# A streaming residual kernel: rows of x read in runs of 16 KB and stored from runs of 8 KB

## The chip, the cores and the metric

The kernel runs on one core of a Trainium2 chip (trn2). The metric is the device time of one execution in microseconds (us); lower is better. The kernel before took 329.73 us, the median of three runs (329.72 to 330.26). All data are float32 in the chip's memory at the start and must be there at the end.

## The reference

There are 128 samples. Each sample is a matrix x[b] of 128 channels by 1024 time steps, and a subject number from 0 to 7 picks one of eight 128 x 128 weight matrices for it:

```python
w = weights[subjects]                            # (128, 128, 128)
out = jnp.einsum('bct,bcd->bdt', x, w)
return x + out                                   # (128, 128, 1024)
```

x is 64 MiB and so is the output; the weights are 0.5 MiB. Every byte of x is read once, and every byte of the output is written once.

## The kernel before, in words

The kernel works on pairs of samples (`G = 2`), so there are `NT = 64` steps. On-chip memory holds 23 slots (`SLOTS`, the tiles `xs`) of one pair each: 128 partitions by 2 x 1024 floats, 1 MB. Channel c of both samples lies in partition c. A step loads a pair into a slot, adds the products to it in place, and stores the slot.

Each engine has its own list of instructions, written out by hand in one critical section; semaphores alone order the engines among each other.

- **SyncE (SP)** issues the 64 loads (L92), in order. From the 24th on it first waits on `s_store[k]` (L91), until the slot's former content has been stored. At the end it waits for the last stores (L138).
- **ScalarE (ACT)** issues the load of the 128 subject numbers (L74), that of all eight weight matrices into `w_all` (L75), and then the 64 stores (L132), each after both samples of its step have been added (`s_added`). Loads are thus on SP's DMA queue (q1 in the profile) and stores on ACT's (q10), with the weights at the head of q10.
- **VectorE** brings the subject numbers into range (L80 to L84), and then makes one addition per sample (L128): product from PSUM plus the slot's content, into the slot.
- **GpSimd (POOL)** waits for the weights (L96), reads a sample's subject number into a register and copies that matrix into one of four small tiles `w0` to `w3` (L112), for each sample in turn.
- **TensorE (PE)** waits for the load of the step (`s_load[k]`, L99) and for the copied matrix (`s_copied`), and multiplies in two halves of 512 columns (L118) into one of four PSUM tiles. Nothing can be multiplied before the weights are there.

A load's access pattern is `"g c t -> c g t"`: for each of 128 partitions two rows of 4 KB, which lie 512 KB apart in memory. The store's pattern is the same in the other direction. Each row is one packet of a DMA engine, and the 128 partitions are spread over the core's 16 DMA engines.

## Time and profile before

| | value |
|---|---|
| median of the runs | 329.73 us |
| the profiled execution's own time | 329.91 us |
| its span, first to last instruction | 328.1 us |
| mean granted TensorE clock | 0.972 |
| TensorE / VectorE / GpSimd busy | 71% / 48% / 12% of the span |
| moved by DMA | 134.86 MB in 35,867 packets, 411 GB/s over the span |
| load of 1 MB, issue to landing (median) | 32.9 us |
| store of 1 MB, issue to landing (median) | 32.3 us |

The span lies inside the run's time; 1.8 us of the profiled execution are outside it. Busy times overlap, since the engines work side by side. The profile's second part cuts the span into 40 slices of 8.2 us and gives each engine's busy share in tenths. Its line DMA is the mean busy share of the 16 DMA engines, and GB/s is what they moved. An issue-to-landing time includes the wait behind earlier transfers of the same queue.

### The profile page before, as it was taken

Reading aid. Unit: us, or ns where it says so; the run is one execution under the profiler, and the core shown is the slowest. Engines: PE = TensorE matmul, PEld = TensorE weight load, DVE = VectorE, ACT = ScalarE, POOL = GpSimd, SP = SyncE. Lnnn points to the kernel's source line nnn. Section 1 sums busy time; section 2 is a strip of 40 time slices with the busy share of each in tenths; the row PEclk is TensorE's granted clock in tenths of the full one; section 3 lists DMA queues with packets and bytes.
Section 4 is the critical chain, followed back from the end, with each engine's and each line's share of the span. In section 5 each row is a group of like instructions: output and inputs, shape, how many; then the busy total and the mean of one; then the engine's idle time right before and its main releaser. Section 6 shows DMA issues by size and latency. Waiting matters only on the chain.

```text
span 328.1 us, 1864 instructions
## 1 busy us (share of the span) xinstructions
PE 233.1 (71%) x512; PEld 94.5 (29%) x512; DVE 157.5 (48%) x131; POOL 37.8 (12%) x132
## 2 busy tenths in 40 slices
PE   0069999999997768768668668677677686686200
PEld 0034444444432322323323223223223233232000
DVE  0017777777775454454454454454554544544200
POOL 0011111111111111111111111111110111110000
PEclk9999999999999999999999999999999999999855
DMA  7999999999999999999999999999999999999995
GB/s 270 391 407 413 422 420 419 423 417 420 423 419 419 422 419 419 420 422 420 420 422 420 421 420 420 420 421 422 419 421 422 417 421 422 421 419 423 421 418 239
DMA packets 35867, 134.86 MB, mean 411 GB/s; under 512 B 2065, under 2 KB 3090, under 8 KB 35858
## 3 DMA queue, kind: packets, MB, share of 16 engines
q10 hardware_dynamic: 18450, 67.64, 50.4%
q1 hardware_dynamic: 17408, 67.11, 50.2%
q8 instruction: 4, 0.07, 0.1%
q14 instruction: 5, 0.04, 0.0%
HBM read 67.63 MB, written 67.11 MB: 411 GB/s over the span
## 4 chain that ended last, share of the span: by engine, by line
SPq 81%; DMA 10%; PE 1%; issue 1%; DVE 0%
SPq L92 81%; DMA x<-in_x_dram 10%; PE ps L118 1%; DVE x L128 0%; SPq L162 0%; SPq L72 0%
## 5 line engine op out<-in xcount | busy, mean ns | idle before, releaser
L118 PE MATMUL ps<-x,w 128*128 128x512 f32 x512 | 233.1, 605 | 72.4 <-DMA x<-in_x_dram 53.3
L128 DVE TENSOR_TENSOR x<-ps,x 128x1024 f32<-128x1024 f32 x128 | 156.8, 1225 | 147.0 <-PE ps L118 147.0
L118 PEld LDWEIGHTS ps<-x,w 128*128 128x128 f32 x512 | 94.5, 191 | 210.2 <-issue 122.1
L112 POOL COPY w<-w_all 128x128 f32 x128 | 37.6, 294 | 257.9 <-PE ps L118 239.2
L80 DVE TENSOR_SCALAR near<-given 1x128 int32<-1x128 int32 x1 | 0.2, 215 | 2.2 <-DMA given<-in_itok_B_dram 2.2
L84 DVE CUSTOM_DVE_ANT_0 index<-near,wrap 1x256 uint16<-1x256 uint16 x1 | 0.3, 280 | 0.0
L82 DVE TENSOR_SCALAR wrap<-near 1x128 int32<-1x128 int32 x1 | 0.2, 216 | 0.0
L153 POOL MEMSET const-float32-0.0<- 128x1 f32 x1 | 0.1, 98 | 0.2 <-issue 0.2
L153 POOL MEMSET const-bfloat16-1.0<- 128x1 bf16 x1 | 0.1, 101 | 0.0
L153 POOL MEMSET const-uint8-127<- 128x1 uint8 x1 | 0.1, 101 | 0.0
L153 POOL MEMSET const-float32-1.0<- 128x1 f32 x1 | 0.1, 98 | 0.0
## 6 DMA issues: line engine op xcount, KB each, us to landing
x<-in_x_dram SPq DMA_DIRECT2D x64, 1024.0 KB, 32.9
out_dram<-x ACTq DMA_DIRECT2D x64, 1024.0 KB, 32.3
w_all<-in_L_cond_weights_dram ACTq DMA_DIRECT2D x1, 512.0 KB, 16.5
given<-in_itok_B_dram ACTq DMA_DIRECT2D x1, 0.5 KB
```

The lines of the kernel that those rows point to most:

```text
L80: nc.vector.tensor_scalar(near, given, -S, S - 1, ALU.max, ALU.min).then_inc(s_index, 1)
L82: nc.vector.tensor_scalar(wrap, near, 0, S, ALU.is_lt, ALU.mult).then_inc(s_index, 1)
L84: nc.vector.tensor_tensor(index, near, wrap, ALU.add).then_inc(s_index, 1)
L92: nc.sync.dma_start(xs[k], x[i * G : (i + 1) * G].rearrange("g c t -> c g t")).then_inc(s_load[k], DMA)
L112: nc.gpsimd.tensor_copy(w, w_all[:, bass.ds(s, 1), :]).then_inc(s_copied, 1)
L118: mm = nc.tensor.matmul(p[:, t : t + N], w[:, 0, :], xs[k][:, g, t : t + N], start=True, stop=True,)
L128: nc.vector.tensor_tensor(xs[k][:, g, :], p, xs[k][:, g, :], ALU.add).then_inc(s_added, 1)
L153: nc = _bacc.Bacc("TRN2", target_bir_lowering=False, num_devices=1)
```

## The change

Loads and stores are built by a new helper, `transfer`, that hands the two sides' access patterns to the instruction as they are, so that the side that is read and the side that is written can be cut into runs of different length.

- **Loads.** There is one load per sample in place of one per pair, so 128 of 512 KB. The source is seen as 32 runs of four rows (`ROWS = 4`), 16 KB each; the destination is still 128 partitions with a row of 4 KB each. Both loads of a slot count on the same semaphore, and matmul waits for both.
- **Stores.** There are still 64 of 1 MB. The source, a slot, is seen as one run of 8 KB per partition (both samples); the destination is still two rows of 4 KB per partition.
- **Allocation.** Tiles come from raw allocations in place of pools.

The loads of the subject numbers and of the weights are as before.

```diff
+ROWS = 4
+QUEUES = {mybir.EngineType.SP: "qSPDynamicHW", mybir.EngineType.Activation: "qActDynamicHW"}
+
+
+def transfer(nc, engine, out, in_):
+    later, nc._always_lower_symbolic_ap = nc._always_lower_symbolic_ap, False
+    ins, outs = engine.lower_ap_dma(in_), engine.lower_ap_dma(out)
+    nc._always_lower_symbolic_ap = later
+    return engine.add_instruction(
+        mybir.InstDMACopy(
+            name=nc.get_next_instruction_name(),
+            engine=engine.engine,
+            ins=ins,
+            outs=outs,
+            mode="Copy",
+            cce_op=ALU.bypass,
+            queue=QUEUES[engine.engine],
+        )
+    )
...
-    xs = [pool.tile([C, G, T], F32, name=f"x{i}") for i in range(SLOTS)]
-    ps = [psum.tile([D, T], F32, name=f"ps{i}") for i in range(P_SLOTS)]
+    xs = [sbuf(f"x{i}", C, G, T) for i in range(SLOTS)]
+    ps = [
+        ctx.enter_context(nc.psum_tensor(f"ps{i}", [D, T], F32)).ap() for i in range(P_SLOTS)
+    ]
...
             if turn:
                 nc.sync.wait_ge(s_store[k], DMA * turn)
-            nc.sync.dma_start(
-                xs[k], x[i * G : (i + 1) * G].rearrange("g c t -> c g t")
-            ).then_inc(s_load[k], DMA)
+            for g in range(G):
+                transfer(
+                    nc,
+                    nc.sync,
+                    xs[k][:, g, :],
+                    x[i * G + g].rearrange("(a r) t -> a (r t)", r=ROWS),
+                ).then_inc(s_load[k], DMA)
...
-            nc.tensor.wait_ge(s_load[k], DMA * (turn + 1))
+            nc.tensor.wait_ge(s_load[k], DMA * G * (turn + 1))
...
-            nc.scalar.dma_start(
-                out[i * G : (i + 1) * G].rearrange("g d t -> d g t"), xs[k]
+            transfer(
+                nc,
+                nc.scalar,
+                out[i * G : (i + 1) * G].rearrange("g d t -> d g t"),
+                xs[k].rearrange("d (o g) t -> d o (g t)", o=1),
             ).then_inc(s_store[k], DMA)
```

More of the change, by code (lines that the diff above doesn't have):

```diff
@@ L49, with sbuf @@
     NT = B // G
-    pool = ctx.enter_context(tc.tile_pool(name="pool", bufs=1))
-    psum = ctx.enter_context(tc.tile_pool(name="psum", bufs=1, space=bass.MemoryType.PSUM))
-    given = pool.tile([1, B], I32, name="given")
-    near = pool.tile([1, B], I32, name="near")
-    wrap = pool.tile([1, B], I32, name="wrap")
-    index = pool.tile([1, B], I32, name="index")
-    w_all = pool.tile([C, S, D], F32, name="w_all")
-    ws = [pool.tile([C, 1, D], F32, name=f"w{i}") for i in range(W_SLOTS)]
-    xs = [pool.tile([C, G, T], F32, name=f"x{i}") for i in range(SLOTS)]
-    ps = [psum.tile([D, T], F32, name=f"ps{i}") for i in range(P_SLOTS)]
+    def sbuf(name, *shape, dtype=F32):
+        return ctx.enter_context(nc.sbuf_tensor(name, list(shape), dtype)).ap()
+    given, near, wrap, index = (
+        sbuf(name, 1, B, dtype=I32) for name in ("given", "near", "wrap", "index")
+    )
+    w_all = sbuf("w_all", C, S, D)
+    ws = [sbuf(f"w{i}", C, 1, D) for i in range(W_SLOTS)]
+    xs = [sbuf(f"x{i}", C, G, T) for i in range(SLOTS)]
+    ps = [
+        ctx.enter_context(nc.psum_tensor(f"ps{i}", [D, T], F32)).ap() for i in range(P_SLOTS)
+    ]
     s_given = tc.alloc_semaphore("s_given")
```

## The prediction

> **What bounds the kernel now.** I read the slices first, then the queues, the chain, the groups and the stage table.

> ```profile
> PEclk9999999999999999999999999999999999999855
> DMA  7999999999999999999999999999999999999995
> GB/s 270 391 407 413 422 420 419 423 417 420 423 419 419 422 419 419 420 422 420 420 422 420 421 420 420 420 421 422 419 421 422 417 421 422 421 419 423 421 418 239
> ...
> q10 hardware_dynamic: 18450, 67.64, 50.4%
> q1 hardware_dynamic: 17408, 67.11, 50.2%
> q8 instruction: 4, 0.07, 0.1%
> q14 instruction: 5, 0.04, 0.0%
> ...
> SPq 81%; DMA 10%; PE 1%; issue 1%; DVE 0%
> ```

> The 16 DMA engines are full in all slices but the first and the last, at 417 to 423 GB/s from the fifth slice on. q1 carries the loads and q10 the stores, and their packets fill 100.6% of the engines' time. The chain lies on SP's queue (81%), which is SP being held in its load instructions until the engines make room. So the span is bytes divided by rate.

> ```profile
> L118 PE MATMUL ps<-x,w 128*128 128x512 f32 x512 | 233.1, 605 | 72.4 <-DMA x<-in_x_dram 53.3
> L128 DVE TENSOR_TENSOR x<-ps,x 128x1024 f32<-128x1024 f32 x128 | 156.8, 1225 | 147.0 <-PE ps L118 147.0
> ...
> w_all<-in_L_cond_weights_dram ACTq DMA_DIRECT2D x1, 512.0 KB, 16.5
> ```

> The stage table's columns are busy time by engine, the TensorE clock, the DMA share and GB/s:

> ```profile
> 18.00:27.00 9.00, 7.87 (x14) 3.54 (x15) 3.02 (x3) 2.05 (x7) 1.00 1.02 409
> 27.00:60.00 33.00, 33.00 (x78) 14.63 (x77) 23.66 (x20) 5.59 (x19) 1.00 1.03 420
> 100.00:200.00 100.00, 74.45 (x162) 28.94 (x161) 49.43 (x41) 11.76 (x40) 1.00 1.02 420
> 299.00:324.00 25.00, 5.20 (x12) 1.82 (x10) 4.71 (x4) 0.00 (x0) 0.71 1.03 421
> 324.00:329.00 5.00, 0.00 (x0) 0.00 (x0) 0.00 (x0) 0.00 (x0) 0.50 0.11 44
> ```

> TensorE is full from 27 to 60 us, while it works off the loads that came in before the weights, then 74% busy. While it catches up, VectorE's adds start every 1.716 us, so compute takes 3.43 us for a slot of two samples; a load and a store of a slot take the DMA 4.99 us. Compute is 30% faster than what binds.

> **One packet's price.** The trace records each packet. With 4 bytes (a semaphore's increment) it lasts 9.0 ns, with 512 bytes (weights) 27.9, with 4 KB 159.1: a line of 0.0366 ns per byte over 9 ns. Four instruction fetches of 8 KB amid the full traffic took 309 ns, as the line says (300 + 9). Records overlap their neighbours, so the occupancy is less: from 60 to 290 us there are 23,589 packets of 4 KB, 1,481 of 4 bytes, and fetches. 230 us x 16 engines, less 1,481 x 9 ns and 5 us of fetches, over 23,589 gives 155.2 ns; the commonest distance between packet starts is 155.3. The bytes cost 150.0 of that, so each packet costs 5.3 ns beside its bytes.

> [...]from 20 to 28 us (4 us bins on the trace's own zero, 12.3 us before the span's) there are 338 load packets of 4 KB per 354 weight packets of 512 B.

> **The change, part by part.**
> (1) Loads. 1 MB is 64 KB for each engine: 16 packets of 4 KB now, 4 of 16 KB after. The bytes, and the rows that one engine takes, are the same. If a packet is what is read as one run, 12 packets x 5.3 ns = 64 ns are saved per load. 16 KB isn't in the trace as an x transfer: by the line it takes 600 + 5.3 = 605 ns.
> (2) Stores. 16 packets become 8 of 8 KB: 8 x 5.3 = 42 ns. Bounds for (1) and (2) together: zero, if the cost is per written row (rows stay 4 KB on both sides); 20 x 9 = 180 ns per pair if the whole 9 ns goes. I take 106, because the 8 KB fetches follow the line.
> (3) One more load instruction per slot: a further 4-byte packet per engine, +9 ns. SP's extra issue is at least 0.42 us (shortest load issue), 64 x 0.42 = 27 us in all; it hides under SP's being held, median 4.63 us an issue. Uncovered it would cost those 27 us.
> Per pair 106 - 9 = 97 ns; 64 pairs make -6.2 us.
> (4) Turns. Weights have 64 packets of 512 B per engine, each taking turns with one load packet. With 605 in place of 155 ns they land 64 x 0.45 = 28.8 us later, at 47 instead of 18 us; the first matmul moves from 19 to 48, the first store's issue from 26 to 55. What covers it is slots: 23 MB at about 2.47 us each last to about 60 us, and longer once stores take turns. Compute then needs 64 x 3.43 = 220 us and ends by 268, well before the end. Without this cover (a smaller number of slots) the delay would stop the DMA. What I charge is 28 us more of the loads-only stretch, which runs at 409 instead of 420 GB/s: 2.6%, +0.7 us.
> (5) Loads at 16 KB a turn against 8 KB for stores win 2:1 until all slots are out, then SP waits on `s_store`. The next loads queue behind that wait and matmul waits for them; but then some twenty finished or unfinished slots lie between, stores are always queued, and the engines stay full. After the last load the stores' tail grows from about 10 slots to some 20; it runs at 421 GB/s, so it costs nothing.
> (6) Raw allocation instead of pools, and the doubled wait count for a load: no instruction on PE, DVE, ACT or POOL is added, and matmuls wait in the same places. Nothing, under the full DMA.

> Sum against the profiled execution: 328.1 - 6.2 + 0.7 = 322.6 us of span; with the 1.8 us outside it (329.9 - 328.1) 324.4. The profiled run lies 0.2 us above the median of 329.73. I forecast 324.5.

> **Rivals.**
> *The price is per written row.* [...]Then nothing is saved and the third semaphore packet is paid: 64 x 9 ns = +0.6, 330.4 us. The same holds if the hardware cuts the runs back to rows.
> *Long packets are slow (slower).* For: the trace's four 16 KB packets[...] took 878 to 960 ns instead of the line's 609, and the 4 KB packets after them 441 and 260. Against: [...]8 KB fetches in the same traffic took 309. At 919 ns a load is 4 x 919 - 4 x 605 = 1.26 us dearer: +80 us, 404. It decides from a 16 KB packet of 605 + 97/4 = 629 ns on, 4% above mine; a mild form, 640 ns, gives 324.4 + 64 x 4 x 0.035 = 333 us.
> *The late weights uncover the DMA.* For: 55 us to the first store's issue, against 60 to the last free slot, and stores need 9.2 us to land. Against: 23 slots, and stores fill the engines once they start. A gap of 3 us gives 327.5. TensorE would bind only if it needed over (319 - 48) / 64 = 4.2 us a slot; the clock stayed at 1.00 from 27 to 290 us.

> **How the numbers follow.** Savings per packet, forecast 324.5 (322 to 327[...], with part of a gap): 0.60. Larger, because the loads-only stretch also speeds up (down to 320.5): 0.06. Gap or part of the savings lost, 327 to 329: 0.06. Per written row, 330.4: 0.13, of which two thirds within 0.2%. Slow long packets: 0.15. About 0.2% (0.7 us) is what a measurement tells from no change. So faster 0.71, same 0.10, slower 0.19. The range 321.0 to 331.5 leaves out the slow packets, and the largest gains.

> **What would show it.** Loads' packets should number 4,096 of 16 KB plus 2,048 semaphores, stores' 8,192 of 8 KB plus 1,024; if rows are recorded instead, the GB/s line decides, which I expect at 428 to 430. The weights' time to landing should go from 16.5 to about 45 us; were it to stay, the turns are still 4 KB and the first rival gains. TensorE should be idle until about 48 us and near full until about 268; SP should wait on the stores. A rate below 420 in the mixed stretch, or load records above 629 ns, would make the forecast wrong, as would an empty DMA slice near 60 us.

## The result, and the profile after

The changed kernel takes 328.10 us (median of four runs, 327.64 to 328.31) against 329.76 us: a ratio of 0.9944, with a 95% interval of 0.9927 to 0.9962. It is faster by 0.56%, where 1.6% was forecast. Its profiled execution took 328.1 us with a span of 326.3, so the span is 1.8 us shorter than before; the forecast was 5.5.

The page of the changed kernel, with the lines that answer to those shown before (slices, queues, chain, TensorE, DMA issues):

```profile
PE   0499999999999888999989887775979877000000
...
DMA  7999999999999999999999999999999999999993
GB/s 268 407 416 422 420 425 419 425 426 423 429 425 421 427 422 428 419 427 424 419 426 420 428 422 434 417 429 423 425 429 426 427 420 425 427 426 427 428 424 164
...
q10 hardware_dynamic: 10258, 67.64, 49.6%
q1 hardware_dynamic: 6144, 67.12, 49.1%
...
x<-in_x_dram SPq DMA_DIRECT2D x128, 512.0 KB, 21.4
out_dram<-x ACTq DMA_DIRECT2D x64, 1024.0 KB, 42.2
w_all<-in_L_cond_weights_dram ACTq DMA_DIRECT2D x1, 512.0 KB, 10.0
```

The change did what it says. q1 now has 6,144 packets (4,096 of 16 KB and 2,048 semaphore increments), where its 17,408 of before were 16,384 rows of 4 KB and 1,024 increments, 16 to a load; and q10 has 8,192 packets of 8 KB beside the weights. The rate rose, but only to about 424 GB/s in the mixed stretch, where I expected 428 to 430. TensorE starts earlier and not later (first matmul at 12.7 us, before at 19.1). And the last slice fell from 239 to 164 GB/s in a span that is shorter: the DMA engines stop further apart than before.

The stage table shows that end best (columns: busy time by compute engine, TensorE clock, DMA share, GB/s). Before:

```profile
318.00:320.00 2.00, 0.00 (x0) 0.00 (x0) 0.00 (x0) 0.00 (x0) 0.50 1.03 424
320.00:322.00 2.00, 0.00 (x0) 0.00 (x0) 0.00 (x0) 0.00 (x0) 0.50 1.03 424
322.00:324.00 2.00, 0.00 (x0) 0.00 (x0) 0.00 (x0) 0.00 (x0) 0.50 1.03 422
324.00:326.00 2.00, 0.00 (x0) 0.00 (x0) 0.00 (x0) 0.00 (x0) 0.50 0.25 102
```

After:

```profile
318.00:320.00 2.00, 0.00 (x0) 0.00 (x0) 0.00 (x0) 0.00 (x0) 0.50 0.97 410
320.00:322.00 2.00, 0.00 (x0) 0.00 (x0) 0.00 (x0) 0.00 (x0) 0.50 0.56 234
322.00:324.00 2.00, 0.00 (x0) 0.00 (x0) 0.00 (x0) 0.00 (x0) 0.50 0.09 37
```

Before, the engines are full until 324 us. After, they begin to run dry at 320, but from 322 to 324 a share of 0.09, which is one and a half engines of 16, still works, and the kernel waits for it.

The trace's packet records give this engine by engine. They do not name the engine, but they fall into 16 sequences in which nearly every packet starts 3 to 4 ns before the record ahead of it ends (99.9% of the packets before and 99.8% after, from 60 to 290 us). Each sequence is taken as one engine and followed back from its last store. The table has the time of an engine's last packet, on the span's clock (to about 0.1 us). The median engine is the middle one of the 16 by that time. "Late" is the last engine less the median one.

| kernel | median engine, us | last engine, us | late, us |
|---|---|---|---|
| before | 324.15 | 325.68 | 1.5 |
| changed | 320.78 | 324.20 | 3.4 |

The median engine is done 3.4 us earlier, the last one only 1.5. In both kernels nine engines end within 0.4 us of each other and seven come later, so the median is one of those that did not lag. There are thus two shortfalls: the packets saved 3.4 us and not 6.2, and 1.9 us of that was lost to engines that lag.

**The packets' price.** The commonest distance between packet starts on one engine is 307 ns for 8 KB stores (most lie between 306 and 310), where two packets of 4 KB took 2 x 155.3 = 310.6, and 613 ns for 16 KB loads beside stores, where four took 621.2. With the bytes at 0.0366 ns (150, 300 and 600 ns) a packet of 4 KB cost 5.3 ns beside its bytes, one of 8 KB 7, one of 16 KB 13. So a longer packet was cheaper per byte (0.0379, 0.0375 and 0.0374 ns), but a part of the price came back as it grew: about a third of what merging two packets should have saved, and half with four. Per pair a load saves 4 x 8.2 = 33 ns, a store 8 x 3.6 = 29, and the extra semaphore costs 9: 53 ns x 64 = 3.4 us, as the median engine has it.

**The lag.** The DMA engines also carry the instruction fetches, packets of 8 KB (queue q14) and 16 KB (q8), eight in mid-run before and nine after. A fetch took time of its own on its engine, and the packet behind it took longer as well. Before, a 16 KB fetch took 878 to 960 ns and the next packet on that engine 441 instead of 159. After, it took 972 to 1,096 ns and a store's packet behind it about 700 instead of 311, or, in one case, a load's packet 1,153 instead of 616. The 8 KB fetches took about 310 ns in both; after, a load's packet behind one took 936 to 1,280 ns. By these records one fetch cost its engine 0.5 to 1.3 us before and 0.5 to 1.6 after. The engines were full from 27 to 318 us (a DMA share of 1.03 before, 1.01 after), so that there was no idle time in which to make that up.

Added up over all fetches this is 7.7 us before; the seven late engines ended together 7.7 us later than the mean of the other nine, so the fetches account for the whole of that lag, and none of it was made up. After, it is 9.4 us, and the late engines' sum is 12.3. Where the other 2.9 us come from stays open.

My theory for the experiments (A) was these two points: packets save less than forecast, and fetches make single engines late. The rivals: each packet saves its 5.3 ns and the gain is lost in the loads-only stretch (B in the first four runs; later B says that fetches don't matter); loads now run up to 23 slots ahead, and the long tail of stores alone loses the gain (C). The slots that loads are ahead of stores are called their lead below.

### The profile page after: what moved, and what is told of

The parts are those of the page before. It is cut to its first block, busy times and chain, and to the rows that moved or that the text cites. A ratio compares the mean times of both kernels' runs of the same rounds, so it can differ in the third digit from the quotient of the medians.

```text
span 326.3 us, 1928 instructions
## 1 busy us (share of the span) xinstructions
PE 237.0 (73%) x512; PEld 97.1 (30%) x512; DVE 157.5 (48%) x131; POOL 37.8 (12%) x132
## 3 DMA queue, kind: packets, MB, share of 16 engines
q10 hardware_dynamic: 10258, 67.64, 49.6%
q1 hardware_dynamic: 6144, 67.12, 49.1%
HBM read 67.63 MB, written 67.11 MB: 413 GB/s over the span
## 4 chain that ended last, share of the span: by engine, by line
DMA 37%; another core or an unknown queue 22%; PE 17%; SPq 7%; DVE 1%; issue 1%; POOLq 0%; ACTq 0%; POOL 0%
DMA out_dram<-x 29%; PE ps L148 17%; SPq L49 7%; DMA x<-in_x_dram 5%; DMA w_all<-in_L_cond_weights_dram 3%; DVE x L158 1%; POOLq L132 0%; ACTq L100 0%; POOLq L142 0%; ACTq L195 0%; POOL w L142 0%; POOLq L126 0%; SPq L98 0%
## 5 line engine op out<-in xcount | busy, mean ns | idle before, releaser
L148 PE MATMUL ps<-x,w 128*128 128x512 f32 x512 | 237.0, 616 | 38.8 <-DMA x<-in_x_dram 26.2
L158 DVE TENSOR_TENSOR x<-ps,x 128x1024 f32<-128x1024 f32 x128 | 156.8, 1225 | 117.3 <-PE ps L148 117.3
L148 PEld LDWEIGHTS ps<-x,w 128*128 128x128 f32 x512 | 97.1, 195 | 177.8 <-issue 122.4
## 6 DMA issues: line engine op xcount, KB each, us to landing
x<-in_x_dram SPq DMA_DIRECT2D x128, 512.0 KB, 21.4
out_dram<-x ACTq DMA_DIRECT2D x64, 1024.0 KB, 42.2
w_all<-in_L_cond_weights_dram ACTq DMA_DIRECT2D x1, 512.0 KB, 10.0
```

The costliest lines, as they stand in the source:

```text
L148: mm = nc.tensor.matmul(p[:, t : t + N], w[:, 0, :], xs[k][:, g, t : t + N], start=True, stop=True,)
L158: nc.vector.tensor_tensor(xs[k][:, g, :], p, xs[k][:, g, :], ALU.add).then_inc(s_added, 1)
```

## The experiments

**Loads alone.** The stores go back to the kernel before's form:

```diff
-            transfer(nc, nc.scalar, out[...], xs[k].rearrange("d (o g) t -> d o (g t)", o=1)).then_inc(...)
+            nc.scalar.dma_start(out[...], xs[k]).then_inc(s_store[k], DMA)
```

> Only the loads are changed (16 KB runs, one sample a load); stores are the kernel before's, with 4 KB runs. Theory A (a packet keeps part of its price for each row that it writes, and single DMA engines that fall behind at instruction fetches set the end): 16 KB load packets at a distance of 613 ns against 4 x 155.3, so 33 ns saved per load and engine, less 9 ns for the second semaphore packet, 64 x 24 ns = 1.6 us, and up to that much given back at the end by the latest engine: 328.2 to 329.8 us. Theory B (each packet saves 5.3 ns, as predicted, and the gain is lost in the loads-only stretch alone): 64 x 55 ns = 3.5 us less 0.7, 326.9 us. Theory C (loads run 23 slots ahead since a load packet is four times a store packet, and the long tail of stores alone loses the gain): no gain or a loss here, 329.8 or above, with the tail as long as in the changed kernel.

Measured: 329.31 us, ratio 0.9981 (0.9973 to 0.9989). The median engine finished at 322.46 us, 1.7 us earlier than before, which is A's saving; the last at 325.77, no earlier than before (325.68). A fits, B's 326.9 doesn't. C's 329.8 or above is missed by only 0.5 us, so the next runs must tell A from C.

**Stores alone.** The loads go back, and with them the count for which matmul waits:

```diff
-            for g in range(G):
-                transfer(nc, nc.sync, xs[k][:, g, :], x[i * G + g].rearrange("(a r) t -> a (r t)", r=ROWS)).then_inc(...)
+            nc.sync.dma_start(xs[k], x[i * G : (i + 1) * G].rearrange("g c t -> c g t")).then_inc(s_load[k], DMA)
```

> Only the stores are changed (8 KB runs); loads are the kernel before's, one of 1 MB per slot with 4 KB runs. Theory A: 8 KB store packets at a distance of 307 ns against 2 x 155.3, 29 ns saved per store and engine, 64 x 29 = 1.9 us: 327.9 us, up to 1 us more if a late engine sets the end. Theory B: 8 x 5.3 = 42 ns, 2.7 us: 327.1 us. Theory C: stores' packets are now twice the loads', so loads run less far ahead than before, the tail is shorter and the whole saving is kept: 327.1 us or below.

Measured: 332.29 us (329.74 to 333.66), ratio 1.0065 (1.0043 to 1.0087). It is slower, and all three theories missed it. Its profiled execution is one of its faster ones (330.43 us). The stage table and the DMA issues of that execution:

```profile
303.00:315.00 12.00, 11.62 (x28) 5.03 (x27) 8.22 (x7) 1.77 (x6) 1.00 1.02 421
315.00:324.00 9.00, 4.51 (x10) 1.44 (x8) 4.03 (x4) 0.00 (x0) 0.98 0.68 282
324.00:329.00 5.00, 0.00 (x0) 0.00 (x0) 0.00 (x0) 0.00 (x0) 0.50 0.39 159
...
x<-in_x_dram SPq DMA_DIRECT2D x64, 1024.0 KB, 32.9
out_dram<-x ACTq DMA_DIRECT2D x64, 1024.0 KB, 9.0
```

A store now lands 9.0 us after its issue, so its queue is nearly empty, while a load waits 32.9. The queues took turns packet by packet: from 30 to 60 us q1 had 1,152 packets and q10 1,133, semaphores counted. A store's packet has twice the bytes of a load's, so stores eat up the loads' lead. The last load lands when nothing is left to hide its product and its store. From 315 us on the engines are 68% and 39% full, and the last matmul starts at 320.4 us, before at 304.9. C had foreseen the shrinking lead and taken it for a gain. No trace shows an execution of 332 or 333 us, so how the slower ones lost more is open.

**Neither side widened.** One load per sample, all runs 4 KB, raw allocation:

```diff
-                transfer(nc, nc.sync, xs[k][:, g, :], x[i * G + g].rearrange("(a r) t -> a (r t)", r=ROWS)).then_inc(...)
+                nc.sync.dma_start(xs[k][:, g, :], x[i * G + g]).then_inc(s_load[k], DMA)
```

(and the stores as in the loads-alone kernel)

> Neither side's runs are widened: one load per sample with 4 KB runs, the kernel before's stores, and raw allocation. Only the doubled load instructions and the allocation are left of the change. All theories: one more semaphore packet of 9 ns per slot and engine, 64 x 9 ns = +0.6 us, 330.3 us; if SP's issues or the allocation cost something of their own, more than 330.6.

Measured: 330.02 us, ratio 1.0005 (0.9997 to 1.0013). The split and the allocation cost 0.15 us, less than the 0.6 expected; the interval allows no more than 0.4.

**Half the slots.**

```diff
-SLOTS = 23
+SLOTS = 12
```

> The changed kernel with 12 slots in place of 23. The loads' lead, and with it the tail of stores alone, is halved (from about 50 us to about 27). Theory A: the packets' prices stay, the latest engine's lag at the end depends on where the fetches fall: 327 to 328.5 us. Theory C: the tail loses half as much as before, about 1.2 us less than the changed kernel, 326.9 us. If slots were what keeps the DMA engines fed, slower than 328.5 us.

Measured: 328.30 us, ratio 0.9950 (0.9937 to 0.9963), beside 328.0 for the changed kernel. The last matmul starts at 302.9 us instead of 275.2, so the tail of stores is more than halved, and nothing is gained: C, with its 326.9, falls. The median engine finished at 320.37 us and the last at 324.76, 4.4 us late.

**The changed kernel again:**

> The changed kernel once more, beside the others of this call. 328.1 us as measured, against 329.8 for the kernel before; the DMA engines should again finish one by one, the last of them some 1.5 to 2 us after the last but one.

Measured: 328.01 us, ratio 0.9941 (0.9927 to 0.9954). Median engine 320.69 us, last 324.25, the last but one 322.2. The lag repeats.

**No product: taking fetches away.** Two kernels, with the transfers of before and with those of the changed kernel. Both leave out the choice and the copy of the weights and the product, so that their output is 2x:

```diff
-                nc.gpsimd.tensor_copy(w, w_all[:, bass.ds(s, 1), :])...   # and the matmuls
-                nc.vector.tensor_tensor(xs[k][:, g, :], p, xs[k][:, g, :], ALU.add)
+                nc.vector.tensor_tensor(xs[k][:, g, :], xs[k][:, g, :], xs[k][:, g, :], ALU.add)
```

> The kernel before's transfers (4 KB runs both ways, 1 MB each) with no work on TensorE and GpSimd: the weights' choice, their copy and the product are left out, and VectorE adds x to itself in place, so that the output is 2x. Few instructions are left, so few of the instruction fetches that go through the same DMA engines. Theory A (fetches make single engines late, and the latest sets the end): the engines finish within 0.5 us of each other instead of 1.7, 328.5 us. Theory B (fetches don't matter): 329.8 us with the old spread.

> The changed kernel's transfers (16 KB loads, 8 KB stores) with the same leaving out as in the 4 KB kernel of this call: output 2x, nothing on TensorE and GpSimd. Theory A: the saving per packet shows whole, 64 x (33 + 29 - 9) ns = 3.4 us less than the 4 KB kernel of this call, so 325.0 us, and the engines finish together. Theory B: the difference to the 4 KB kernel stays at 1.7 us, as between the changed kernel and the kernel before.

Measured: 328.81 us with 4 KB runs (ratio 0.9968, 0.9957 to 0.9979), 326.25 with the wide ones (0.9890, 0.9874 to 0.9905). The difference is 2.6 us, between A's 3.4 and B's 1.7; the second kernel missed A's 325.0 by 1.2 us. The end of the 4 KB one (columns: VectorE, GpSimd, clock, DMA share, GB/s):

```profile
322.00:324.00 2.00, 0.00 (x0) 0.00 (x0) 1.00 0.95 389
324.00:326.00 2.00, 0.00 (x0) 0.00 (x0) 1.00 0.02 8
```

and of the wide one:

```profile
318.00:320.00 2.00, 0.00 (x0) 0.00 (x0) 1.00 0.98 414
320.00:322.00 2.00, 0.00 (x0) 0.00 (x0) 1.00 0.23 94
322.00:324.00 2.00, 0.00 (x0) 0.00 (x0) 1.00 0.01 4
```

Most engines now stop together. With 4 KB runs the mid-run fetches are down to one, of 8 KB; the median engine ended at 323.90 us, the last at 324.73. With wide runs there are two; 14 engines ended within 0.4 us around 320.36, one 0.75 us later and one, at 322.47, 2.1 us later. The median engines differ by 3.5 us: the packets' saving, again as A has it. One engine's 2.1 us is more than the single 8 KB fetches there explain: with the packets behind them they took 1.0 and 0.6 us. Where the rest comes from stays open. These kernels take away more than fetches, so the next run adds fetches alone.

**Adding fetches.**

```diff
                 nc.gpsimd.tensor_copy(w, w_all[:, bass.ds(s, 1), :]).then_inc(s_copied, 1)
+                for j in range(6):
+                    nc.gpsimd.memset(spare[:, 6 * b + j : 6 * b + j + 1], 0.0)
```

> The changed kernel with six tiny memsets of a spare tile added on GpSimd after each sample's weights are copied: 768 more instructions on an engine that is busy for 12% of the span, and so more instruction fetches through the DMA engines. Theory A (each fetch makes one DMA engine late for good, and the latest engine sets the end): the engines finish further apart than 3.8 us, or the same if the new fetches fall on engines that were early; 328.5 to 330.5 us. Theory B (fetches don't matter): 328.0 us.

Measured: 329.84 us, ratio to before 0.9996 (0.9988 to 1.0004), 1.8 us above the changed kernel. The queue line and the end of this kernel:

```profile
q14 instruction: 11, 0.09, 0.1%
...
320.00:322.00 2.00, 0.00 (x0) 0.00 (x0) 0.00 (x0) 0.00 (x0) 0.50 0.49 205
322.00:324.00 2.00, 0.00 (x0) 0.00 (x0) 0.00 (x0) 0.00 (x0) 0.50 0.14 57
324.00:326.00 2.00, 0.00 (x0) 0.00 (x0) 0.00 (x0) 0.00 (x0) 0.50 0.09 37
```

q14 has 11 packets instead of 5, 0.05 MB more in 134.9. The median engine ended at 320.89 us, within 0.1 of the changed kernel's 320.78; the last at 326.08 instead of 324.20. GpSimd was 19% busy; TensorE's last matmul started at 277.4 us instead of 275.2, long before the end. By the records all fetches, with the packets behind them, took 12.9 us of single engines' time instead of 9.4. So 50 KB of fetches took back the whole gain: the median engine kept its saving, and the last one lost it. That fetches make engines late is thereby shown in both directions; the size of the lateness is not, since part of it stays open.

**8 KB loads.**

```diff
-ROWS = 4
+ROWS = 2
```

> The changed kernel with loads of two rows a run, 8 KB, in place of four. Theory A (part of a packet's price goes with each written row): an 8 KB load packet takes 307 ns as the stores' do, so a load costs 8 x 307 = 2456 ns against 4 x 613 = 2452, and next to nothing of the saving is lost; a fetch holds up the packet behind it for less; turns are even, so loads run less far ahead: 327 to 328.5 us. If the price went with the packet alone (predicted: 5.3 ns each), 4 more packets per load would cost 21 ns, 1.4 us: 329.5 us.

Measured: 330.32 us, ratio 1.0012 (1.0005 to 1.0018). The packets' distance is 307 ns, as A expected, and the rate is that of the changed kernel until near the end, where it breaks off:

```profile
GB/s 255 410 408 430 426 425 425 426 424 423 427 427 420 431 425 420 428 428 422 424 428 427 421 430 426 420 429 427 424 426 428 422 425 425 426 423 430 425 295 160
...
x<-in_x_dram SPq DMA_DIRECT2D x128, 512.0 KB, 39.9
out_dram<-x ACTq DMA_DIRECT2D x64, 1024.0 KB, 13.5
```

A's 327 to 328.5 us is missed. It is the lost lead again: stores land in 13.5 us, loads in 39.9, and the last matmul starts at 321.0 us. Packets of both queues have 8 KB here, but a slot's loads need 10 turns for their 8 data packets (two semaphore packets), a store 9. The trace has it so: from 60 to 100 us there are 988 data packets on q1 and 1,085 on q10, but with the semaphores 1,236 and 1,229.

**Keeping the lead.** Two kernels, stores alone widened and 8 KB both ways, each with a wait on ScalarE:

```diff
             nc.scalar.wait_ge(s_added, (i + 1) * G)
+            if i + LEAD < NT:                      # LEAD = 10
+                j = i + LEAD
+                nc.scalar.wait_ge(s_load[j % SLOTS], DMA * G * (j // SLOTS + 1))
```

(without the factor G where a slot has one load)

> The kernel with only the stores widened (8 KB runs, loads of 4 KB runs), which took 332.29 us, plus one wait: the store of a slot is held on ScalarE until the load ten slots later has landed, so that loads keep the lead that they have in the kernel before. Theory D (the loss was the loads' lost lead, which bared the last slot's load, product and store at the end): the packets' saving of 64 x 29 ns comes back, 328 to 329 us. Rival E (8 KB stores beside 4 KB loads are themselves slow): it stays at 331 us or above.

> The kernel with 8 KB loads and 8 KB stores, which took 330.32 us, plus the same wait that keeps loads ten slots ahead. Theory D: it loses the bared end, 2 us or more, and 8 KB packets cost per byte what the 16 KB ones do: 327 to 328.3 us, as fast as the changed kernel or a little faster. Rival E (loads need runs of 16 KB to gain): above 329 us.

Measured: 330.12 us (ratio 0.9996, 0.9986 to 1.0007) and 328.27 (0.9958, 0.9944 to 0.9972), 2.2 and 2.05 us below the same kernels without the wait. So keeping the lead wins back 2 us in both; the first doesn't come down to the expected 328 to 329. The second one's stage table says what is still missing:

```profile
285.00:295.00 10.00, 7.40 (x16) 2.87 (x16) 4.90 (x5) 0.59 (x2) 1.00 0.95 397
295.00:303.00 8.00, 3.70 (x8) 1.44 (x8) 2.83 (x3) 0.00 (x0) 1.00 0.85 348
303.00:315.00 12.00, 0.00 (x0) 0.00 (x0) 0.00 (x0) 0.00 (x0) 0.52 1.01 419
```

While the last loads run out, stores are still held. The first kernel has the same hole, with a DMA share of 0.73 from 295 to 303 us.

**Letting the last stores go.**

```diff
-            if i + LEAD < NT:
+            if i + LEAD < NT - 4:
```

> The kernel with 8 KB loads and stores in which a store is held until the load ten slots later has landed (328.27 us), but the last stores are let go: no hold once the load waited for would be one of the last four. In the held form the DMA engines are 85% and 95% full for some 18 us near the end, as the last loads run while stores are held, about 1.9 us of lost time. Theory D: that comes back, and the median engine finishes where the changed kernel's does, with less lateness of single engines since the holds had them wait for each other: 326.3 to 327.3 us, faster than the changed kernel's 328.0. Rival: single engines' lateness adds up again over the rest of the run, as in the changed kernel, and the end stays at 328 us.

Measured: 328.07 us, ratio 0.9947 (0.9933 to 0.9960). The hole is closed:

```profile
285.00:295.00 10.00, 6.90 (x16) 2.87 (x16) 4.83 (x4) 0.88 (x3) 1.00 1.01 426
295.00:303.00 8.00, 4.20 (x10) 1.44 (x8) 3.72 (x4) 0.00 (x0) 1.00 1.01 425
```

and the time is still that of the changed kernel. The median engine ended at 321.60 us, 0.8 later than the changed kernel's, and the last at 324.87, 3.3 us late: the rival of that run was right, lateness adds up again. In the four kernels whose queues ran dry near the end (stores alone, 8 KB loads, and the two with the full wait) all 16 engines ended within 0.3 us of each other, so there the late ones had caught up while the others had nothing to do. No kernel of the study that computes the whole result beats the changed one clearly.

## Why the prediction was off

- **What bounds it** was right: the DMA engines were full through mid-run (from 60 to 190 us a DMA share of 1.03 before and 1.01 after), and the price of a packet is what the change moves.
- **Steps (1) and (2), the packets' saving**: this is the term that failed. I let the whole 5.3 ns beside a packet's bytes vanish with each packet merged: 64 + 42 = 106 ns per pair. Measured: 33 + 29 = 62. Longer packets do not follow the line through 4 bytes, 512 bytes, 4 KB and the 8 KB fetches; the 16 KB load is 613 ns and not 605. A fixed price for every packet, whatever its length, is thus not what the runs show, if the bytes cost 0.0366 ns. Why is open. That the remainder goes with the written rows, as my first rival had it whole, was only argued, and the 0.13 that I gave that rival was an estimate: no run varied rows and run length apart, and 5.3, 7 and 13 ns do not rise evenly with a run's one, two and four rows. A rival that I had not named fits as well, by an estimate from two of these figures: a line through the distances of 4 and 16 KB (155.3 and 613 ns) has 2.7 ns a packet and 0.0373 ns a byte, and gives 308 for 8 KB. Then the error was to take the bytes' price from the records of short packets. My lower and upper bounds (0 and 180) held the truth; I took the value of 8 KB fetches for loads and stores in runs of 8 and 16 KB.
- **Step (3), semaphore and issues**: 9 ns is the length of a semaphore packet's record, but the next packet starts 5 to 6 ns after its start, so the split should cost 0.4 us and not 0.6. As a whole it cost 0.15 us, and SP's issues were hidden.
- **Step (4), late weights**: wrong in sign. They landed 10.0 us after their issue, not 45, and not the 16.5 of before. The trace's packet records show why: the first load is now only two packets per engine, done about 2 us after the first transfer began, and the weights were then all but alone on the engines: 865 of their 1,024 packets ran from 3.8 to 5.8 us, and 16 of the loads'. The turns that I had multiplied were not taken, as the loads' queue had next to no packets then. My charge of 0.7 us for a longer stretch of loads alone didn't fall due either, since the first store was issued at 20.4 us, before at 26.0.
- **Step (5), turns**: right in kind. From 60 to 100 us q1 and q10 had 938 packets each, but semaphores among them, so that loads won 1.5:1 in bytes (621 packets of 16 KB against 826 of 8 KB) and not 2:1. On an engine, 1,858 of 1,878 packets were followed by one of the other queue. Loads ran ahead until the slots were out, SP waited on stores for 116.5 us, stores took 42.2 us to land, and the longer tail of stores by itself costs nothing, as 12 slots showed. What I missed is what it is worth: with 4 KB loads the same turns went to the stores and lost 2.4 us.

The line of the waits of SP's queue after (us in total, times, longest):

```profile
SPq L49 <- DMA out_dram<-x: 116.5, 28, 5.1
```

- **The sum** treated 16 engines as one rate. It had no term for the last engine. Its lateness grew from 1.5 to 3.4 us: 3.4 - 1.9 = 1.5 us at the last packet, and 0.3 us less between that and the span's end make the 1.8. The time fell into the case "gap or part of the savings lost", to which I had given 0.06; there was no gap, and the lagging engines were not in my argument.
- **The rivals**: long packets were a little slow (613), below the 629 ns from which I had the change turn slower. The instruction fetches that I brought up as a sign of slow packets were a cause of their own, by the 0.5 to 1.6 us that one took from the engine that carried it. With 768 more GpSimd instructions q14's 8 KB fetches went from 5 to 11, and q8's 16 KB ones stayed at four.

## What to carry to other kernels

In a kernel that is bound by DMA, count packets with the price of the very shape that they will have, not with a line through others, and don't count on the whole fixed cost: here 62 ns a pair came back of 106. With two queues on the same engines, count bytes per turn, and a semaphore packet as a turn: here loads of 16 KB won 1.5:1 in bytes beside stores of 8 KB, while stores of 8 KB cost loads of 4 KB their lead (332.29 us), and even loads of 8 KB (330.32). Widen loads more than stores, or keep the loads' lead by a wait (2 us won back in both kernels), so that the last load isn't bare at the end. And look at when each DMA engine stops, not only at the rate: six more fetches of 8 KB cost this kernel 1.8 us.
